# Spreading a row factor with GpSimd's partition broadcast, after the product, in the x3 stage of a four-layer kernel

## The chip, the cores and the metric

The kernel runs on one core of a Trainium2 chip. The core has five engines with a queue of instructions each: TensorE (PE; its weight loads are listed apart as PEld), VectorE (DVE), ScalarE (ACT), GpSimd (POOL) and SyncE (SP), which here only issues transfers. Sixteen DMA engines carry out the transfers. Data is worked on in SBUF, 128 partitions wide; TensorE writes its products to PSUM, from which VectorE and ScalarE read.

The metric is the device time of one execution in microseconds (us). Before the change the median of three runs is 3373.68 us, from 3369.82 to 3382.41.

## The reference, cut to what matters

The input is x, 256 x 256 tokens of 128 channels in fp32. Four layers follow one another, each of the form x = x + layer(group_norm(x)): an attention over rows, a triangle product with 16 channels, a triangle product with 128 channels, and a convolution. The change lies in the third, layer 2:

```python
zn = _layernorm(z, ln_in_w, ln_in_b)
a = jax.nn.sigmoid(zn @ Wga + bga) * (zn @ Wla + bla)
b = jax.nn.sigmoid(zn @ Wgb + bgb) * (zn @ Wlb + blb)
k = jnp.einsum('bimc,bmjc->bijc', a, b)
out = jax.nn.sigmoid(zn @ Wgo + bgo) * (_layernorm(k, ln_o_w, ln_o_b) @ Wlo + blo)
```

Here z is the group-normalised x2 (x after two layers), and x3 = x2 + out. The last line is what the changed stage computes. A layer norm takes a mean and a factor (one over the standard deviation) per token. The kernel folds the subtraction of the token's mean, and the norm's weights, into the weight matrices; what is left for each token is a subtraction of the group norm's mean per channel, and a multiplication by one number per token.

## The kernel before, in words

Activations are kept in HBM with channels as rows: x2T, kD and x3T are 128 rows of 65,536 tokens. The work is done in 32 blocks of SC = 2048 tokens (1 MB), each in two halves of H2 = 1024, each half in two pieces of CK = 512, the width of one product in PSUM. Every stage is written under manual scheduling: each engine gets its instructions in the order of the program text, and a tile pool with n buffers makes the writer of a tile wait for the last reader of the tile n before it.

Layer 2 has three stages. The first (p5, lines 1091 to 1230) makes a and b, the row rs2D of token factors, and, for the last two blocks only, the finished gates (`gates`). The second (p6, lines 1251 to 1288) multiplies them into kD, collecting the sums of k and of k squared in k1 and k2. The third, called the x3 stage here (p7, lines 1292 to 1394), is the one that is changed. For each block s it

- loads k (`load7k`, four buffers) and x2 (`load7x`, seven buffers in two pools);
- spreads two rows of factors over the 128 partitions with `broadcast_rows`: four matmuls with K = 32, whose weights pick row s out of a tile that holds all blocks' factors as [32 c + s, 512]; the rows are rs2 (factor of z, `normalise_z`) and rk (factor of k, `normalise_k`). The spread rows stand in PSUM, in the pool psX, which has two buffers of two banks;
- multiplies them in on VectorE: lines 1318 (z, with the mean m2 subtracted first) and 1310 (k);
- takes the gate product on TensorE and its sigmoid on ScalarE (`gate7`, three blocks ahead of use, AHEAD = 3), then the product of k (`product7`), both into the pool psM with two buffers of two banks;
- multiplies gate and product on VectorE (line 1379), adds x on GpSimd (line 1392), sums x3 and its square on ScalarE for the next group norm (`sums7`, lines 1338 and 1339) and stores the block (`finish7`, line 1344).

In iteration s the order on TensorE is: gate product of block s + 3, half 0; k product of block s, half 0; z broadcast of block s + 4; gate product, half 1; k product, half 1; k broadcast of block s + 1. VectorE follows it with the gate times product of half 0, the z multiplies, the gate times product of half 1, and the k multiplies. GpSimd has one addition of the whole block. The sync queue issues the load of k for block s + 3, the load of x for block s + 5 and the store of block s - 1, in that order; the x load reuses the buffer of block s - 2. Blocks 30 and 31 have their gates already, so from iteration 26 on there is no z broadcast, and from 27 on no gate product.

Ahead of the loop come the z multiplies of blocks 0 to 3, the root and reciprocal of k's variance (lines 1350 to 1355), its way through HBM into rk (lines 1356 to 1358), the gates of blocks 0 to 2 and the first k multiply.

Of the kernel before, what the change touches and what calls it, by code (L numbers as in the profile page):

```python
# [2 lines left out]

# [5 lines left out]

F32 = mybir.dt.float32  # L10
AF = mybir.ActivationFunctionType
ALU = mybir.AluOpType
# [4 lines left out]
P = 128  # L17
# [3 lines left out]
SC = 2048  # L21
NSC = T // SC
CK = 512
# [9 lines left out]
def kernel(ctx: ExitStack, tc: tile.TileContext, a: dict, out: bass.AP):  # L33
    nc = tc.nc
# [22 lines left out]
    rs2D = dram.tile([1, T], F32, name="rs2D")  # L57
# [13 lines left out]
    const = ctx.enter_context(tc.tile_pool(name="const", bufs=1))  # L71
# [20 lines left out]
    for sign, base in ((1, 0), (-1, 3)):  # L92
# [2 lines left out]
            pattern=[[-4 * sign, 32], [0, 4]], channel_multiplier=sign,  # L95
        )
    gmat = gmat.rearrange("p a b -> p (a b)")
    epst = const.tile([P, 1], F32, name="epst")
    nc.vector.memset(epst, EPS)

# [45 lines left out]
    b2w = const.tile([P, 6], F32, name="b2w")  # L146
# [91 lines left out]
    with tc.tile_pool(name="x0", bufs=1) as xres, tc.tile_pool(name="p0", bufs=3) as sb:  # L238
        held = {s: xres.tile([P, SC], F32, name=f"x0_{s}") for s in range(RES, NSC)}
        with tc.tile_pool(name="p0ps", bufs=3, space=PSUM) as ps, tc.tile_pool(  # L240
            name="f0ps", bufs=2, space=PSUM
# [167 lines left out]
        with tc.tile_pool(name="p1", bufs=2) as wk_sb, tc.tile_pool(  # L409
            name="p1ps", bufs=4, space=PSUM  # L410
# [8 lines left out]
            with tc.manual_schedule():  # L419
# [5 lines left out]
                for i, s in enumerate(order):  # L425
# [4 lines left out]
                    for c in range(4):  # L430
                        nc.tensor.matmul(
                            pr[32 * c : 32 * c + 32, :], lhsT=wt, rhs=xc[:, c * CK : (c + 1) * CK],
                            start=True, stop=True,
# [17 lines left out]
                    while len(sums) > (i < NSC - 1):  # L451
                        j, sq = sums.pop(0)
                        for c in range(4):
                            nc.tensor.matmul(
                                e2[32 * c : 32 * c + 32, :], lhsT=slide[:, 31 - j : 63 - j],
                                rhs=sq[:, c * CK : (c + 1) * CK], start=(j == order[0]), stop=(j == order[-1]),
# [24 lines left out]
    with tc.tile_pool(name="p2e", bufs=6) as eb, tc.tile_pool(name="p2c", bufs=1) as cs:  # L481
        triT = cs.tile([P, NH, 2, N], F32, name="triT")
        with tc.tile_pool(name="p2", bufs=2) as sb, tc.tile_pool(
            name="p2S", bufs=2, space=PSUM
        ) as psS, tc.tile_pool(name="p2z", bufs=1, space=PSUM) as psZ, tc.tile_pool(
            name="p2M", bufs=3, space=PSUM
# [183 lines left out]
            rb = psS.tile([P, 2, CK], F32, name="p2i_rb", tag="p2_S")  # L670
            for c in range(2):
                nc.tensor.matmul(
                    rb[:, c, :], lhsT=sel[32 * c : 32 * c + 32, 0:1].to_broadcast([32, P]),
                    rhs=rs0[32 * c : 32 * c + 32, :], start=True, stop=True,
# [173 lines left out]
    with x1_scope:  # L848
        with tc.tile_pool(name="p3", bufs=3) as sb, tc.tile_pool(
            name="p3ps", bufs=3, space=PSUM  # L850
# [15 lines left out]
            for i, s in enumerate(order1):  # L866
                p1 = ps.tile([P, CK], F32, name="p3_1")
                p2 = ps.tile([P, CK], F32, name="p3_2")
                for pp, w in ((p1, v1), (p2, v2)):
                    for c in range(4):  # L870
                        nc.tensor.matmul(
                            pp[32 * c : 32 * c + 32, :], lhsT=w, rhs=xs[s][:, c * CK : (c + 1) * CK],
                            start=True, stop=True,
# [18 lines left out]
        with tc.tile_pool(name="z", bufs=2) as sb, tc.tile_pool(  # L892
            name="zps", bufs=3, space=PSUM
# [28 lines left out]
            at = turn_z(0)  # L922
            for k in range(16):
                nxt = turn_z(k + 1)
                pz = tri_multiply(nc, ps, at, AB[k // 2][1], k % 2).rearrange("p t n -> p (t n)")
                at = nxt
# [32 lines left out]
        with tc.tile_pool(name="p4", bufs=3) as sb, tc.tile_pool(  # L959
            name="p4psg", bufs=2, space=PSUM  # L960
        ) as psg, tc.tile_pool(name="p4psz", bufs=2, space=PSUM) as psz, tc.manual_schedule():
            zs, gts, sums = {}, {}, []
# [42 lines left out]
            for i, s in enumerate(order):  # L1005
# [5 lines left out]
                for c in range(4):  # L1011
# [3 lines left out]
                        start=True, stop=True,  # L1015
# [54 lines left out]
    with tc.tile_pool(name="f2", bufs=1) as sb, tc.tile_pool(name="f2ps", bufs=1, space=PSUM) as ps:  # L1070
        po = ps.tile([P, 1], F32, name="f2_o")
        nc.tensor.matmul(po, lhsT=ones, rhs=mr2neg, start=True, stop=True)
        nc.vector.tensor_scalar(off2, po, 1.0 / D, None, ALU.mult)

    H2 = 2 * CK

    def broadcast_rows(psX, rows, s, name, tag="x"):


        rb = [psX.tile([P, 2, CK], F32, name=name, tag=tag) for _ in range(2)]  # L1080
        for c in range(4):
            nc.tensor.matmul(  # L1082
                rb[c // 2][:, c % 2, :], lhsT=sel[32 * c : 32 * c + 32, s : s + 1].to_broadcast([32, P]),
                rhs=rows[32 * c : 32 * c + 32, :], start=True, stop=True,
            )
        return [t.rearrange("p c t -> p (c t)") for t in rb]
# [4 lines left out]
    rs2_scope = ExitStack()  # L1091
# [140 lines left out]

    rk_pool = rs2_scope.enter_context(tc.tile_pool(name="rk", bufs=1))
    x7_pool = rs2_scope.enter_context(tc.tile_pool(name="x7", bufs=3))
    z7_pool = rs2_scope.enter_context(tc.tile_pool(name="z7", bufs=2))
    rk = rk_pool.tile([P, CK], F32, name="rk")
    rs2 = rk_pool.tile([P, CK], F32, name="rs2_")
    for c in range(4):
        nc.gpsimd.dma_start(  # L1239
            rs2[32 * c : 32 * c + 32, :], rs2D.rearrange("o (s c t) -> c (o s) t", c=4, t=CK)[c]  # L1240
        )
    k1 = rk_pool.tile([P, 2 * N], F32, name="k1")
    k2 = rk_pool.tile([P, 2 * N], F32, name="k2")
    xs7 = {}
# [1 line left out]
    def load7x(s, pool, bufs):  # L1246
        if s < NSC:
            xs7[s] = pool.tile([P, SC], F32, name="p7_x", bufs=bufs)
            nc.sync.dma_start(xs7[s], x2T[:, s * SC : (s + 1) * SC])

    with tc.tile_pool(name="p6", bufs=3) as sb, tc.tile_pool(name="p6ps", bufs=3, space=PSUM) as ps:
        nc.vector.memset(k1, 0.0)
# [41 lines left out]
    with tc.tile_pool(name="p7", bufs=2) as sb, tc.tile_pool(name="p7psX", bufs=2, space=PSUM) as psX, tc.tile_pool(  # L1294
        name="p7psM", bufs=2, space=PSUM
    ) as psM, tc.manual_schedule():
        ks, zns, gts = {}, {}, dict(gates)
        AHEAD = 3

        def load7k(s):  # L1300
            if s < NSC:
                ks[s] = sb.tile([P, SC], F32, name="p7_k", bufs=4)
                nc.sync.dma_start(ks[s], kD[:, s * SC : (s + 1) * SC])

        def normalise_k(s):
            if s < NSC:
                rb = broadcast_rows(psX, rk, s, "p7_rk")
                for h in range(2):
                    hs = slice(h * H2, (h + 1) * H2)
                    nc.vector.tensor_tensor(ks[s][:, hs], rb[h], ks[s][:, hs], ALU.mult)  # L1310

        def normalise_z(s):
            if s < NSC and s not in gates:
                rb = broadcast_rows(psX, rs2, s, "p7_rz")
                zns[s] = z7_pool.tile([P, SC], F32, name="p7_zn")
                for h in range(2):
                    hs = slice(h * H2, (h + 1) * H2)
                    nc.vector.scalar_tensor_tensor(
                        zns[s][:, hs], xs7[s][:, hs], m2, rb[h], ALU.subtract, ALU.mult
                    )  # L1320

        def product7(src, w, h):
            pm = psM.tile([P, 2, CK], F32, name="p7_pm")
            for c in range(2):
                k = 2 * h + c
                nc.tensor.matmul(pm[:, c, :], lhsT=w, rhs=src[:, k * CK : (k + 1) * CK], start=True, stop=True)  # L1326
            return pm.rearrange("p c t -> p (c t)")

        def gate7(s, h):
            if s < NSC and s not in gates:  # L1330
                if h == 0:
                    gts[s] = sb.tile([P, SC], F32, name="p7_g", bufs=5)
                nc.scalar.activation(
                    gts[s][:, h * H2 : (h + 1) * H2], product7(zns[s], wf2[:, 4, :], h), AF.Sigmoid, bias=b2w[:, 4:5]
                )

        def sums7(x, junk, i):
            nc.scalar.activation(junk, x, AF.Identity, bias=m2neg, accum_out=g1[:, i : i + 1])
            nc.scalar.activation(junk, x, AF.Square, bias=m2neg, accum_out=g2[:, i : i + 1])

        def finish7(s):
            x = xs7.pop(s)
            sums7(x, gts.pop(s), s)
            nc.sync.dma_start(x3T[:, s * SC : (s + 1) * SC], x)

        load7k(0)
        load7x(3, sb, 4)
        normalise_z(0)

        nc.vector.scalar_tensor_tensor(k1, k1, -1.0 / D, k1, ALU.mult, ALU.mult)  # L1350
        nc.vector.tensor_tensor(k2, k2, k1, ALU.add)
        nc.vector.tensor_scalar(k2, k2, 0.0, None, ALU.max)
        nc.scalar.activation(k2, k2, AF.Sqrt, bias=epst, scale=1.0 / D)
        normalise_z(1)
        nc.vector.reciprocal(k1, k2)
        nc.sync.dma_start(rkD.rearrange("o (p t) -> p (o t)", p=P), k1)
        for c in range(4):
            nc.sync.dma_start(rk[32 * c : 32 * c + 32, :], rkD.rearrange("o (s c t) -> c (o s) t", c=4, t=CK)[c])
        for s in range(1, 3):
            load7k(s)  # L1360
        load7x(4, sb, 4)
        gate7(0, 0)
        gate7(0, 1)
        normalise_z(2)
        gate7(1, 0)
        gate7(1, 1)
        normalise_z(3)
        gate7(2, 0)
        gate7(2, 1)
        normalise_k(0)  # L1370
        for s in range(NSC):
            load7k(s + 3)
            load7x(s + 5, *((x7_pool, 3) if (s + 5) % 7 < 3 else (sb, 4)))
            last = s == NSC - 1
            for h in range(2):
                hs = slice(h * H2, (h + 1) * H2)
                gate7(s + AHEAD, h)
                pl = product7(ks[s], w2[:, 5, :], h)
                nc.vector.scalar_tensor_tensor(gts[s][:, hs], pl, b2w[:, 5:6], gts[s][:, hs], ALU.add, ALU.mult)  # L1379
                if h == (s + AHEAD not in gates and s + AHEAD < NSC):  # L1380
                    normalise_k(s + 1)
                if h == 0:
                    normalise_z(s + AHEAD + 1)
                if last:
                    nc.vector.tensor_tensor(xs7[s][:, hs], xs7[s][:, hs], gts[s][:, hs], ALU.add)
                    if h == 0:
                        finish7(s - 1)
                    sums7(xs7[s][:, hs], gts[s][:, hs], s + h)
                    nc.sync.dma_start(x3T[:, s * SC + h * H2 : s * SC + (h + 1) * H2], xs7[s][:, hs])
            del ks[s]  # L1390
            if not last:
                nc.gpsimd.tensor_tensor(xs7[s], xs7[s], gts[s], ALU.add)  # L1392
                if s:
                    finish7(s - 1)
# [486 lines left out]
```

## Time and profile before

| what | value |
|---|---|
| median of three runs | 3373.68 us (3369.82 to 3382.41) |
| profiled execution, first to last instruction (its own time and its span are this one figure) | 3369.3 us |
| TensorE busy, whole span | 3117.7 us, 93% |
| VectorE, ScalarE, GpSimd busy | 2268.5, 2019.0, 1593.4 us |
| mean granted TensorE clock | 0.962 |
| HBM traffic | 458.35 MB read, 287.64 MB written |
| x3 stage: first z broadcast, first product of the loop, last sum | 2628.34, 2650.33, 2939.5 us |
| x3 stage, 2750 to 2800 us: PE, DVE, ACT, POOL busy | 50.00, 38.01, 33.45, 22.72 of 50 us |

The page of the profile shows one execution on the chip. Line numbers are those of the kernel before. A group of instructions reads: line, engine, operation, written tile <- read tiles, shapes, count, then busy time, mean time of one in ns, and the engine's idle time just before them with what ended it. In the profile's names digits that follow a letter's prefix are left out, so p7_rz is p_rz, p7_pm is p_pm and p7_x is p_x; names such as p_x and p_pm occur in other stages as well. An fp32 product appears as two matmul records of 512 columns, so a half of a block (two products) is four, and the four broadcast matmuls are eight, which run side by side on four groups of 32 rows. The chain of work that ended last is followed backwards from the last instruction, at each step to what released it.

### The profile page before, as it was taken

How to read it: one execution, taken by the hardware profiler on the slowest of the kernel's cores; microseconds unless marked ns; L12 is line 12 of the kernel's file. 1: busy time of each engine (PE TensorE's matmuls, PEld its weight loads, DVE VectorE, ACT ScalarE, POOL GpSimd, SP SyncE). 2: the span in 40 equal slices, each digit the busy share in tenths (PEclk: the TensorE clock that was granted, in tenths of full speed). 3: DMA queues.
4: the chain of work that ended last, by engine and by line, in shares of the span. 5: the costliest groups of instructions: out<-in, count | busy, mean ns of one | idle time of the engine just before them, and what ended most of it. 6: DMA issues, size and time to landing. Idle time of an engine off the chain costs nothing. (4 is left out here: it accounts for less than half of the span.)

```text
span 3369.3 us, 52577 instructions
## 1 busy us (share of the span) xinstructions
PE 3117.7 (93%) x20274; PEld 1644.3 (49%) x20274; DVE 2268.5 (67%) x2612; ACT 2019.0 (60%) x2209; POOL 1593.4 (47%) x878
## 2 busy tenths in 40 slices
PE   6669999999999999967997999999999999769998
PEld 5415555555555555523432444445999433224444
DVE  5627888888888888853555455444555677758776
ACT  3657777777777777734686444443444466636565
POOL 4146777777777777720483000001555344414444
PEclk8889999999999999988997999999999999979999
DMA  9972333333333333369597768666999899756764
GB/s 395 366 292 81 121 109 121 108 121 109 120 109 117 112 113 116 108 262 351 196 408 306 264 244 315 244 237 254 350 352 352 305 335 332 283 159 201 211 188 132
DMA packets 297977, 749.51 MB, mean 222 GB/s; under 512 B 74585, under 2 KB 145195, under 8 KB 248571
## 3 DMA queue, kind: packets, MB, share of 16 engines
q1 hardware_dynamic: 289659, 735.24, 61.2%
q0 software_dynamic: 7776, 9.81, 0.9%
q8 instruction: 162, 2.65, 0.3%
q10 hardware_dynamic: 288, 1.05, 0.1%
q14 instruction: 92, 0.75, 0.1%
HBM read 458.35 MB, written 287.64 MB: 221 GB/s over the span
## 5 line engine op out<-in xcount | busy, mean ns | idle before, releaser
L564 DVE TENSOR_TENSOR p_e<-p_S,triT 128x1024 f32<-128x1024 f32 x512 | 609.3, 1212 | 144.4 <-PE p_S L554 144.4
L574 POOL TENSOR_TENSOR p_es<-p_e 128x1024 f32<-128x1024 f32 x256 | 603.5, 2368 | 125.3 <-issue 65.3
L572 ACT ACTIVATE p_e<-p_e,mbT 128x1024 f32<-128x1024 f32 x512 | 551.8, 1137 | 61.4 <-DVE p_e L564 61.3
L1167 PE MATMUL p_pm<-p_zn,wf 128*128 128x512 f32 x1040 | 449.6, 593 | 2.1 <-ACT p_a L1202 1.9
L539 PE MATMUL p_mm<-p_xn,w 128*128 128x512 f32 x768 | 405.3, 611 | 0.3 <-DVE p_v L534 0.3
L1167 PEld LDWEIGHTS p_pm<-p_zn,wf 128*128 128x128 f32 x1040 | 196.5, 190 | 255.3 <-issue 246.1
L554 PE MATMUL p_S<-p_q,p_k 32*128 32x256 f32 x4096 | 295.4, 400 | 3.5 <-DVE p_e L564 3.3
L1575 POOL TENSOR_TENSOR p_q<-p_q,p_pb 128x2024 f32<-128x2024 f32 x32 | 144.2, 4506 | 254.3 <-DVE p_pb L1569 254.3
L554 PEld LDWEIGHTS p_S<-p_q,p_k 32*128 32x128 f32 x4096 | 185.9, 184 | 159.5 <-PE p_mm L530 91.7
L1839 PE MATMUL tp_z<-p_B,tp_at 128*128 128x256 f32 x1024 | 250.5, 388 | 0.8 <-DMA p_B<-bD 0.5
L587 PE MATMUL p_o<-p_e,p_v 128*32 128x256 f32 x4096 | 248.6, 383 | 0.0
L513 POOL TENSOR_TENSOR p_xn<-p_xn,p_rs 128x1024 f32<-128x1024 f32 x63 | 151.4, 2403 | 205.5 <-DMA p_rb<-rzD 114.2
L1239 POOL DMA_DIRECT2D rs__17906<-rs2D x4 | 2.0, 510 | 506.5 <-DVE p_zn L1160 506.5
L1282 POOL TENSOR_TENSOR k<-k,p_sq 128x512 f32<-128x512 f32 x128 | 163.2, 1275 | 156.8 <-ACT p_sq L1280 156.8
L1392 POOL TENSOR_TENSOR p_x<-p_x,p_g 128x2048 f32<-128x2048 f32 x30 | 136.4, 4547 | 160.4 <-DVE p_g L1379 87.4
L1839 PEld LDWEIGHTS tp_z<-p_B,tp_at 128*128 128x128 f32 x1024 | 185.1, 191 | 23.2 <-DVE tp_at L1830 1.6
L539 PEld LDWEIGHTS p_mm<-p_xn,w 128*128 128x128 f32 x768 | 126.0, 190 | 104.6 <-issue 88.5
L1281 DVE TENSOR_TENSOR k<-tp_z,k 128x512 f32<-128x512 f32 x128 | 88.6, 692 | 127.1 <-ACT p_sq L1280 127.1
L587 PEld LDWEIGHTS p_o<-p_e,p_v 128*32 128x32 f32 x4096 | 120.3, 110 | 110.3 <-ACT p_g L545 41.5
L1278 ACT COPY p_K<-tp_z 128x512 f32<-128x512 f32 x128 | 75.1, 587 | 157.9 <-PE tp_z L1839 157.9
L545 ACT ACTIVATE p_g<-p_mm,bgh 128x512 f32<-128x512 f32 x128 | 88.0, 687 | 131.4 <-PE p_mm L539 131.3
L530 PEld LDWEIGHTS p_mm<-w,p_xn 128*128 128x128 f32 x1024 | 134.4, 191 | 61.1 <-issue 60.4
(379 smaller groups left out, 5892.7 us busy)
## 6 DMA issues: line engine op xcount, KB each, us to landing
p_x<-x2T SPq DMA_DIRECT2D x60, 1024.0 KB
x<-x1T SPq DMA_DIRECT2D x51, 1024.0 KB
p_x<-in_x_dram SPq DMA_DIRECT2D x32, 1024.0 KB
p_x<-xT SPq DMA_DIRECT2D x64, 512.0 KB
x2T<-x SPq DMA_DIRECT2D x32, 1024.0 KB
aD<-p_a SPq DMA_DIRECT2D x32, 1024.0 KB
bD<-p_b SPq DMA_DIRECT2D x32, 1024.0 KB
p_A<-aD SPq DMA_DIRECT2D x32, 1024.0 KB
```

Of the source, the lines that this page charges most:

```text
L513: nc.gpsimd.tensor_tensor(xn, xn, groups[g]["rs"], ALU.mult)
L539: nc.tensor.matmul(pm, lhsT=w, rhs=t["xn"][:, cs_], start=True, stop=True)
L554: nc.tensor.matmul(Ss[h // 2][:, h % 2, u, :], lhsT=t["k"][hp, r * N + u * P : r * N + (u + 1) * P], rhs=t["q"][hp, r * N : (r + 1) * N], ...
L564: nc.vector.tensor_tensor(e[:, :, 2 * p : 2 * p + 2, :].rearrange("p u h n -> p h u n"), Ss[p], triT[:, 2 * p : 2 * p + 2, :, :], ALU.add,)
L572: nc.scalar.activation(e[:, u, :, :], e[:, u, :, :], AF.Exp, bias=mbT[:, u, i : i + 1])
L574: nc.gpsimd.tensor_tensor(es, e[:, 0, :, :], e[:, 1, :, :], ALU.add)
L587: nc.tensor.matmul(t["o"][hp, r % 2, :], lhsT=t["v"][:, r * 2 + u, hp], rhs=e[:, u, h, :], start=(u == 0), stop=(u == 1),)
L1167: nc.tensor.matmul(pm[:, c, :], lhsT=wf2[:, i, :], rhs=zns[s][:, k * CK : (k + 1) * CK], start=True, stop=True)
L1282: nc.gpsimd.tensor_tensor(k2, k2, sq, ALU.add)
L1392: nc.gpsimd.tensor_tensor(xs7[s], xs7[s], gts[s], ALU.add)
L1575: nc.gpsimd.tensor_tensor(q[:, :, 1 : N - 2], q[:, :, 1 : N - 2], pb[:, :, 0 : N - 3], ALU.add)
L1839: nc.tensor.matmul(pz[:, t, :], lhsT=at[:, u, t * P : (t + 1) * P], rhs=Bc[:, u, :], start=(u == 0), stop=(u == 1))
```

## The change

The z factor is no longer spread by TensorE and no longer multiplied onto x before the gate product. The gate product now takes x2 as it was loaded. The factor row of a block is loaded as one row of 2048 numbers into partition 0, 32, 64 or 96 of the tile rs2 (`row7`), right behind the load of x; GpSimd's partition broadcast writes it to all 128 partitions of a tile rbs in SBUF (`spread_z`, two buffers). VectorE then computes (product + gcol) times the spread row into a tile zg, and ScalarE takes the sigmoid from there. gcol is the product of the gate weights with the negative mean, one column, made once ahead of the x2 stage by one more matmul and copy.

The k factor is still spread by TensorE, but now in `spread_k` right after the k product of half 0, and the two halves are multiplied separately: half 0 behind the first gate times product of an iteration, half 1 behind the second.

The row tile no longer comes by four GpSimd transfers of the whole factor tile. A library with the partition broadcast is loaded to GpSimd near the start of the kernel, ahead of the weights' transfers. In the start of the stage the k statistics now come before anything else on VectorE, since no z multiply stands ahead of them.

```diff
     gmat = gmat.rearrange("p a b -> p (a b)")
+    nc.gpsimd.load_library(library_config.all_libraries[10])
...
+        pg = ps.tile([P, 1], F32, name="f2_g")
+        nc.tensor.matmul(pg, lhsT=wf2[:, 4, :], rhs=m2neg, start=True, stop=True)
+        gcol = const.tile([P, 1], F32, name="gcol")
+        nc.vector.tensor_copy(gcol, pg)
...
-    z7_pool = rs2_scope.enter_context(tc.tile_pool(name="z7", bufs=2))
-    rs2 = rk_pool.tile([P, CK], F32, name="rs2_")
-    for c in range(4):
-        nc.gpsimd.dma_start(
-            rs2[32 * c : 32 * c + 32, :], rs2D.rearrange("o (s c t) -> c (o s) t", c=4, t=CK)[c]
-        )
+    rs2 = rk_pool.tile([P, SC], F32, name="rs2_")
+
+    def row7(s):
+        at = 32 * (s % 4)
+        return rs2[at : at + 1, :]
...
             nc.sync.dma_start(xs7[s], x2T[:, s * SC : (s + 1) * SC])
+            nc.sync.dma_start(row7(s), rs2D[:, s * SC : (s + 1) * SC])
...
-        def normalise_k(s):
+        def spread_k(s):
             if s < NSC:
-                rb = broadcast_rows(psX, rk, s, "p7_rk")
-                for h in range(2):
-                    hs = slice(h * H2, (h + 1) * H2)
-                    nc.vector.tensor_tensor(ks[s][:, hs], rb[h], ks[s][:, hs], ALU.mult)
-
-        def normalise_z(s):
+                rks[s] = broadcast_rows(psX, rk, s, "p7_rk")
+
+        def normalise_k(s, h):
+            if s < NSC:
+                hs = slice(h * H2, (h + 1) * H2)
+                nc.vector.tensor_tensor(ks[s][:, hs], rks[s][h], ks[s][:, hs], ALU.mult)
+
+        def spread_z(s):
             if s < NSC and s not in gates:
-                rb = broadcast_rows(psX, rs2, s, "p7_rz")
-                zns[s] = z7_pool.tile([P, SC], F32, name="p7_zn")
-                for h in range(2):
-                    hs = slice(h * H2, (h + 1) * H2)
-                    nc.vector.scalar_tensor_tensor(
-                        zns[s][:, hs], xs7[s][:, hs], m2, rb[h], ALU.subtract, ALU.mult
-                    )
+                rbs[s] = sb.tile([P, SC], F32, name="p7_rb")
+                nc.gpsimd.partition_broadcast(rbs[s], row7(s))
...
         def gate7(s, h):
             if s < NSC and s not in gates:
+                hs = slice(h * H2, (h + 1) * H2)
                 if h == 0:
                     gts[s] = sb.tile([P, SC], F32, name="p7_g", bufs=5)
-                nc.scalar.activation(
-                    gts[s][:, h * H2 : (h + 1) * H2], product7(zns[s], wf2[:, 4, :], h), AF.Sigmoid, bias=b2w[:, 4:5]
-                )
+                pg = product7(xs7[s], wf2[:, 4, :], h)
+                zg = sb.tile([P, H2], F32, name="p7_zg")
+                nc.vector.scalar_tensor_tensor(zg, pg, gcol, rbs[s][:, hs], ALU.add, ALU.mult)
+                nc.scalar.activation(gts[s][:, hs], zg, AF.Sigmoid, bias=b2w[:, 4:5])
...
-        normalise_z(0)
+        spread_z(0)
+        spread_z(1)
...
-        normalise_z(1)
...
-        gate7(0, 0)
-        gate7(0, 1)
-        normalise_z(2)
-        gate7(1, 0)
-        gate7(1, 1)
-        normalise_z(3)
-        gate7(2, 0)
-        gate7(2, 1)
-        normalise_k(0)
+        for s in range(3):
+            gate7(s, 0)
+            gate7(s, 1)
+            if s < 2:
+                spread_z(s + 2)
+        spread_k(0)
+        normalise_k(0, 0)
+        normalise_k(0, 1)
...
-                if h == (s + AHEAD not in gates and s + AHEAD < NSC):
-                    normalise_k(s + 1)
                 if h == 0:
-                    normalise_z(s + AHEAD + 1)
+                    spread_k(s + 1)
+                    spread_z(s + AHEAD + 1)
+                normalise_k(s + 1, h)
```

More of the change, by code (lines that the diff above doesn't have):

```diff
@@ L5 @@
 import concourse.tile as tile
-from concourse import mybir
+from concourse import library_config, mybir
 from concourse.masks import make_identity
@@ L1296 @@
     ) as psM, tc.manual_schedule():
-        ks, zns, gts = {}, {}, dict(gates)
+        ks, rks, rbs, gts = {}, {}, {}, dict(gates)
         AHEAD = 3
```

## The prediction

> **What bounds the kernel now.** I began with the row of 40 slices on the page, to see which engine is full where, and with the chain of work that ended last. The x3 stage runs from about 2628 to 2939 us of the 3369.3 us span, slices 32 to 35 (of 84.2 us). The lines are TensorE (PE) and DMA busy tenths:
>
> ```profile
> PE   6669999999999999967997999999999999769998
> ...
> DMA  9972333333333333369597768666999899756764
> ```
>
> In those slices TensorE stands at 9, and the DMA engines at 8, 9, 9, 7: two candidates. The chain, asked for a stretch in the middle of the stage (start, length, what), decides:
>
> ```profile
> 2744.42 3.63 PE p_pm L1326 x8
> 2748.05 1.07 PE p_rz L1082 x8
> 2749.12 3.63 PE p_pm L1326 x8
> 2752.75 1.07 PE p_rk L1082 x8
> 2753.82 3.63 PE p_pm L1326 x8
> ```
>
> No other engine and no transfer appears in it: it is TensorE's own instructions back to back. One block of 2048 tokens takes 3.63 + 1.07 + 3.63 + 1.07 = 9.40 us: two pairs of products (gate and k, one pair per half) and two row broadcasts, one of the z factor (p_rz), one of the k factor (p_rk). The windows view of the same stage (busy us of PE, PEld, DVE, ACT, POOL, then clock, DMA share, GB/s; the last line is an earlier stage):
>
> ```profile
> 2750.00:2800.00 50.00, 50.00 (x171) 18.73 (x173) 38.01 (x33) 33.45 (x32) 22.72 (x5) 1.00 0.94 340
> ...
> 1684.00:1769.00 85.00, 84.27 (x281) 31.09 (x280) 49.26 (x74) 70.72 (x69) 70.14 (x23) 1.00 1.01 409
> ```
>
> TensorE is busy for 50.00 of 50 us at full clock. VectorE has 24% free, GpSimd half. DMA is 94% busy but moves only 340 GB/s, where the same queue moved 409 GB/s in the earlier stage, with its megabyte loads and stores; so I do not read 0.94 as full. The groups of the stage (line, engine, tiles, count, busy, mean ns, idle before and why) give the prices:
>
> ```profile
> L1392 POOL TENSOR_TENSOR p_x<-p_x,p_g 128x2048 f32<-128x2048 f32 x25 | 113.6, 4545 | 147.9 <-DVE p_g L1379 75.0 <-DMA x3T<-p_x 72.9
> ...
> L1379 DVE SCALAR_TENSOR_TENSOR p_g<-p_pm,b2w,p_g 128x1024 f32<-128x1024 f32 x51 | 65.5, 1284 | 56.1 <-PE p_pm L1326 56.1
> L1318 DVE SCALAR_TENSOR_TENSOR p_zn<-p_x,gn_mean,p_rz 128x1024 f32<-128x1024 f32 x50 | 61.6, 1273 | 0.0
> L1310 DVE TENSOR_TENSOR p_k<-p_rk,p_k 128x1024 f32<-128x1024 f32 x52 | 61.0, 1214 | 2.3 <-PE p_rk L1082 2.3
> L1333 ACT ACTIVATE p_g<-p_pm,b2w 128x1024 f32<-128x1024 f32 x52 | 58.0, 1114 | 83.7 <-PE p_pm L1326 83.0
> ```
>
> VectorE's and ScalarE's idle time ends in a TensorE product: both wait for TensorE. And the sync queue's loads and stores of one block, from the order of time:
>
> ```profile
> 2752.78 0.32 SPq L1303 DMA_DIRECT2D p_k<-kD  x1
> 2756.32 0.32 SPq L1249 DMA_DIRECT2D p_x<-x2T  x1
> 2758.86 0.32 SPq L1344 DMA_DIRECT2D x3T<-p_x  x1
> ```
>
> **What the Trainium skill says.** "GPSIMD Engine Reference", section 3.1, gives 4497 ns for a two-input add at 2048 fp32 elements; L1392 shows 4545 ns, so it agrees. The same section gives 1.03 cycles an element at 1.2 GHz for short one-input loops; no run here shows one of this size. Its section 2.1 adds about 6 us at the first call of a freshly loaded library; not shown here either. "SBUF — State Buffer", section on the two sides, says that GpSimd and VectorE exclude each other only when VectorE reads two SBUF inputs or runs a two-port mode. The trace agrees as far as it goes: L1379 reads PSUM and SBUF, and takes 1.28 us beside a running L1392 as well as without. The new VectorE instruction has that form too.
>
> **The change part by part.**
>
> *z broadcasts on TensorE, removed.* In the loop normalise_z ran for s + 4 below 30, so in 26 iterations, each 1.07 us of the chain. A block falls from 9.40 to 8.33 us: 26 x 1.07 = 27.8 us. Cover is needed from every other resource below 8.33 us a block:
>
> *VectorE.* Two L1318 go, two scalar_tensor_tensor of PSUM product, column and spread row come, the same form at about 1.28 us. Sum per block 2 x (1.28 + 1.28 + 1.21) = 7.54 us; 0.8 us free. Order matters more: products alternate between two PSUM buffers, and now VectorE frees all of them. Laying out one block from 0: gate product 0 to 1.81, k product to 3.62, k broadcast to 4.69, gate to 6.50, k to 8.31. VectorE's second gate multiply then starts at 6.6 and ends at 7.9; its buffer is wanted at 8.31. The second k multiply ends at 9.75; its buffer is wanted at 10.1. It fits with 0.4 us to spare; if lost, what is late is the next gate product, by the difference. k's halves are scaled half a block earlier than used, so the 0.42 us for which weight loads waited on L1310 is gone too, without worth.
>
> *ScalarE.* The sigmoid moves behind VectorE. ScalarE spends 2 x 1.11 on it and 2 x 2.19 on the sums, 6.6 us a block; gates are made three blocks ahead, so a later sigmoid delays nobody.
>
> *GpSimd.* One broadcast of 2048 elements joins the 4.55 us add. No row shows it. From below: the one-input rate, 2048 x 1.03 / 1.2 GHz = 1.8 us (estimate). From above: a two-input pass over the same tile, 4.55 us. I take 2.5 us: one pass, plus handing the row from core to core. 4.55 + 2.5 = 7.05, under 8.33, so hidden; from 3.8 us up it isn't. It is queued between two adds: behind it wait the next add, the x3T store and, through the sync queue, the x load. The row for block s + 4 is asked for one iteration before its broadcast and used one iteration after, which leaves over a microsecond.
>
> *DMA.* Thirty-two row loads of 8 KB go onto the sync queue, 0.32 us of issue each, three of them before the stage, under the products of p6; the four GpSimd loads of rs2 (L1239, 2.0 us in all, long before use) go. In a block the queue issues 4 x 0.32 = 1.3 us. Data per block 3.15 MB: at 8.33 us that is 378 GB/s, above today's 340, below 409 (7.7 us). The sync queue is in order: the x load waits until an x3T store has landed and ScalarE's sums have left its buffer, and behind it stand the row load and the next store. In before a store is issued at 2749.5 (one block ahead of 2758.86) and the x load that waits for it at 2756.3, under 7 us; that loop fits in 8.33 us, barely. x has more slack than before: its first reader is the gate product, half a block later than L1318 was. Cost nothing; both ends for the range: 0, and the DMA rival below.
>
> *Start of the stage.* Before: first z broadcast at 2628.34, two z multiplies ahead of the k statistics on VectorE, reciprocal at 2636.18, four z broadcasts among six gate products, loop entered at 2650.33. After: the statistics come first; the chain is last GpSimd sum 2628.98, k2 add 0.69, max 0.43, root 0.72, reciprocal 3.34, so the first gate multiply at about 2634.6. Its first two products are long done by then (slow clock: eight passes in 5.85 us there). Four more at about 1.8 to 2.4, and the k broadcast at 1.07, give loop entry near 2645.5. Gain 4.5 us; 2 if the first broadcast pays 6 us.
>
> *End of the stage.* From block 27 on there is no gate; k halves are now apart, so the second gate of block 27 comes some 0.6 us earlier than at 2910.4 and the GpSimd adds behind it follow. Gain 0.5.
>
> *Elsewhere.* One product and copy for gcol before the x2 stage: 0.3 us lost. The library load stands ahead of the weights' DMAs on GpSimd at 3.4 us; the tightest weights (the w2 columns, issued by 52.5) are first read at 67 us, so 6 us hides; without that cover it would cost as much as it exceeds 12.
>
> Sum: 27.8 + 4.5 + 0.5 - 0.3 = 32.5 us. From the profiled 3369.3: 3336.8. The median of the runs shown, 3373.7, is 4.4 above that execution, so 3341 for a median.
>
> **The rivals.**
>
> *DMA becomes the bound.* For: 0.94 busy now. If that is truly full, 340 / 0.94 = 362 GB/s, 8.7 us a block, 26 x 0.7 = 18 us, and with the start and about 3 us of loads in advance some 23; with 350 GB/s, 9.0 us and 15. 3350 to 3359. Against: 409 GB/s above.
>
> *GpSimd becomes the bound.* A broadcast of 4.55 us gives 9.1 us a block: 26 x 0.3 = 8, with a start gain of 2: 3364. For: nothing in the trace prices it. Against: it reads one row and has one input.
>
> *Slower: the broadcast is a slow cross-partition operation.* It decides from 9.40 - 4.55 = 4.85 us per row. The skill's GPSIMD page, section 3.2, has a reduction over partitions of this size at 247.7 us (no run here shows it). At 10 us a block takes 14.55 us: 26 x 5.15 = 134 us more, 3508. Against: a copy has no arithmetic across partitions.
>
> *The change does not do what it says:* TensorE would still issue p_rz; the diff leaves it no such instruction in this stage. No chance given.
>
> **How the numbers follow.** Sum as worked out (a block at 8.3 to 8.5 us): 0.70, its own range 3332 to 3350, being 26 x 0.17 = 4 us on one side and the start's 2 us and the spread of the runs (3369.8 to 3382.4) on both. DMA: 0.13. GpSimd bound: 0.09. Slow broadcast: 0.08. The bound of same is 0.5%, 17 us, about what a measurement of this kernel can tell from no change. Faster: 0.70 and most of the DMA case, 0.79. Same: its rest and the GpSimd case, 0.13. Slower: 0.08. The range reaches from 3329 over the DMA case to 3364, at the GpSimd case.
>
> **What would show it.** Right: chain of 3.63 and 1.07 with only p_rk, starts of L1326 pairs repeating every 8.33 us; GpSimd under 7.5 us a block; 375 GB/s or more; loop entry at about 17 us from the first product. Wrong: TensorE waiting for VectorE's gate multiply (buffers), VectorE for the spread row (GpSimd), or products for x (DMA); or the first 100 us, or GpSimd's L574 in the attention, longer than before.

## The result

The changed kernel is slower. Its median is 3427.68 us (3423.35 to 3430.35), beside 3374.31 us (3369.82 to 3382.41) for the kernel before on the same chip: a ratio of 1.0139, 95% interval 1.0102 to 1.0175. The forecast was 3341 us.

The profiled execution has a span of 3421.6 us, 52.3 more than before. Two marks divide it: the last store of k at the end of p6, and the first instruction of the group norm behind the x3 stage.

| stretch | before, us | after, us | difference |
|---|---|---|---|
| start to the last k store | 2627.1 | 2640.2 | +13.1 |
| x3 stage, to the group norm's statistic | 312.9 | 354.4 | +41.5 |
| from there to the end | 429.3 | 427.0 | -2.3 |

The 40 slices of the page of after (TensorE and DMA busy tenths, slices of 85.5 us), in answer to the same two lines of before:

```profile
PE   5669999999999999967996999999999987759998
...
DMA  9982333333333333378697676767998877756764
```

In slices 32 to 35, those of the stage, TensorE stands at 9, 8, 7, 7 and DMA at 8, 7, 7, 7. In before they were 9, 9, 9, 7 and 8, 9, 9, 7: TensorE had a 7 in slice 35 then too, in which the stage ends, and not 9 throughout as the prediction read it. In slices 33 and 34 neither is full any more. The windows view of after (busy us of PE, PEld, DVE, ACT, POOL, then clock, DMA share, GB/s) has one stretch near the start of the loop and one a little later:

```profile
2663.00:2687.00 24.00, 24.00 (x72) 9.34 (x71) 21.17 (x18) 12.45 (x11) 16.84 (x6) 1.00 0.92 342
2703.00:2763.00 60.00, 47.02 (x123) 17.95 (x122) 38.49 (x32) 34.95 (x35) 37.99 (x11) 0.92 0.77 263
```

In the first, TensorE is busy for 24.00 of 24 us. In the second for 47.02 of 60, and the DMA engines move 263 GB/s at a share of 0.77. Something changed in between. The chain of the work that ended last shows what (start, length, what; the kernel after):

```profile
2664.77 7.07 PE p_pm L1329 x16
2671.84 1.07 PE p_rk L1087 x8
...
2690.72 10.37 DMA x3T<-p_x
...
2701.17 0.32 SPq L1254
...
2701.87 11.21 DMA x3T<-p_x
```

The first two lines are what was forecast: the products of a block and one broadcast, 7.07 + 1.07, 8.13 us from block to block, with the z broadcast gone. From 2690.72 on the chain is a transfer, the store of x3, then the load of x that waits for it, and the next store, which takes 11.21 us. TensorE is no longer in it. The groups of the stage after (line, engine, tiles, count, busy, mean ns, idle before and why) clear the compute engines:

```profile
L1339 DVE SCALAR_TENSOR_TENSOR p_zg<-p_pm,gcol,p_rb 128x1024 f32<-128x1024 f32 x60 | 76.9, 1283 | 78.6 <-PE p_pm L1329 74.2 <-POOL p_x L1396 4.4
...
L1323 POOL PARTITION_BROADCAST p_rb<-rs__17908 x30 | 68.7, 2294 | 103.7 <-DMA rs__17908<-rs2D 62.2 <-DMA p_x<-x2T 32.9 <-DVE p_zg L1339 4.6
```

The new broadcast takes 2.29 us, VectorE's new form 1.28. GpSimd idles for transfers, VectorE for TensorE, and TensorE for 52.6 us for the x load. The order of time on the sync queue shows the change of regime (start, issue time, transfer; L1254 loads x, L1349 stores x3, L1309 loads k):

```profile
2681.54 0.32 SPq L1254 DMA_DIRECT2D p_x<-x2T  x1
...
2682.60 0.32 SPq L1349 DMA_DIRECT2D x3T<-p_x  x1
...
2689.94 0.32 SPq L1254 DMA_DIRECT2D p_x<-x2T  x1
...
2690.72 0.32 SPq L1349 DMA_DIRECT2D x3T<-p_x  x1
2692.84 0.32 SPq L1309 DMA_DIRECT2D p_k<-kD  x1
2701.17 0.32 SPq L1254 DMA_DIRECT2D p_x<-x2T  x1
...
2701.87 0.32 SPq L1349 DMA_DIRECT2D x3T<-p_x  x1
...
2713.13 0.32 SPq L1254 DMA_DIRECT2D p_x<-x2T  x1
```

At 2681.54 the x load goes out 1.06 us ahead of the store. The store of 2690.72 then has the x load and the k load in flight beside it, and lands 10.37 us later. The x load of 2701.17 needs that landing, because it reuses the buffer that the store reads. And the next store, 2701.87, stands behind the x load in the queue, though its data were ready: GpSimd's addition had ended at 2698.85. From there x load, store and k load (the latter at 2702.30) go out within 1.2 us, and nothing more is issued until the store has landed: a round of 11.96 us here, 11.7 on average over the 22 rounds from 2701.17 to the last x load at 2958.51. I call this the lock. What the sync queue waits for in the stage (us in total, times, longest), after:

```profile
SPq L1254 <- DMA x3T<-p_x: 235.5, 25, 10.6
```

and before:

```profile
SPq L1249 <- DMA x3T<-p_x: 39.7, 25, 2.7
SPq L1249 <- ACT p_g L1339: 39.6, 25, 3.0
```

Before, an x load waited 39.7 / 25 = 1.6 us for the store and then another 1.6 us for ScalarE's sums. The queue came to that wait when the k load had gone out (2752.78 + 0.32, with the store ahead of it at 2749.45), so the store had landed about 3.7 + 1.6 = 5.3 us after its issue. After, it waits 9.4 us on average, nearly always for the store.

In the first 13.1 us of the difference the start of the kernel has a part. In the kernel after GpSimd waits without a releaser that the profile shows, ahead of the identity matrix:

```profile
11.13 0.28 POOL masks.py:199 TENSOR_SCALAR_AFFINE_SELECT ident<-ident 128x128 f32<-128x128 f32 x1 [9.96 <-issue]
```

A second such wait, 5.00 us long, ends at 18.29, where the new library is loaded. TensorE's first transposes wait for that identity, until 11.47 us, where before they began at 6.00:

```profile
11.47 4.99 PE L336 MATMUL p_t<-ident,p_x 128*128 128x128 f32 x24 [11.47 <-POOL ident masks.py:199]
```

### The profile page after: what moved, and what is told of

Its sections match the earlier page's. It is cut to its first block, busy times and chain, and to the rows that moved or that the text cites. A ratio compares the mean times of both kernels' runs of the same rounds, so it can differ in the third digit from the quotient of the medians.

```text
span 3421.6 us, 52156 instructions
## 1 busy us (share of the span) xinstructions
PE 3105.4 (91%) x20036; PEld 1648.5 (48%) x20036; DVE 2273.1 (66%) x2613; ACT 2021.0 (59%) x2209; POOL 1659.4 (48%) x904
## 3 DMA queue, kind: packets, MB, share of 16 engines
q10 hardware_dynamic: 288, 1.05, 0.1%
## 5 line engine op out<-in xcount | busy, mean ns | idle before, releaser
L1329 PE MATMUL p_pm<-p_x,wf 128*128 128x512 f32 x240 | 131.2, 677 | 58.8 <-DMA p_x<-x2T 52.6
L588 PEld LDWEIGHTS p_o<-p_e,p_v 128*32 128x32 f32 x4096 | 120.0, 109 | 109.3 <-ACT p_g L546 41.5
```

The lines of the kernel that those rows point to most:

```text
L588: nc.tensor.matmul(t["o"][hp, r % 2, :], lhsT=t["v"][:, r * 2 + u, hp], rhs=e[:, u, h, :], start=(u == 0), stop=(u == 1),)
```

## The experiments

Two theories stood first. Theory Q: the in-order sync queue, in which a load that waits for a store's landing holds up the next store. Theory R: the 32 row loads. For the start, theory L: the library load is on the path.

**The row loads left out, all but four.**

```diff
-            nc.sync.dma_start(row7(s), rs2D[:, s * SC : (s + 1) * SC])
+            if s < 4:
+                nc.sync.dma_start(row7(s), rs2D[:, s * SC : (s + 1) * SC])
```

> The changed kernel, but only the first four factor rows are loaded; the 28 later row loads are left out, so later blocks are multiplied with old rows. Theory Q (the sync queue locks: the x load waits for the store of the block before, that store stands behind the x load, and all transfers of a block run together, so that the store lands last): the rows are a small part of it, the loop still locks at 11 to 12 us a block, time 3410 to 3425. Theory R (the single-partition row load holds up one DMA engine, which runs on alone for some 2.5 us in each block): without the rows the loop goes at 8.1 to 8.5 us a block, time 3345 to 3360 (the 13 us lost ahead of the stage stay).

3428.52 us, ratio 1.0152 (1.0133 to 1.0172), as slow as after; the sync queue waits 233.1 us in 24 waits for x3 stores, as in after. Theory R falls as the reason for the loss.

**The store ahead of the x load.**

```diff
             load7k(s + 3)
-            load7x(s + 5, *((x7_pool, 3) if (s + 5) % 7 < 3 else (sb, 4)))
...
                 if s:
                     finish7(s - 1)
+            load7x(s + 5, *((x7_pool, 3) if (s + 5) % 7 < 3 else (sb, 4)))
```

> The changed kernel, with the loads of x and of the row issued after the store of the same iteration instead of before it; nothing left out. Theory Q: the store no longer stands behind the x load, so it lands before the next x load needs it; 8.1 to 8.6 us a block, 3345 to 3365. Theory R: the row still holds up an engine and the store with it; 10 us a block or more, 3390 or more.

3349.67 us, ratio 0.9932 (0.9909 to 0.9955): faster than before, with the same work and the same engines as after. The sync queue of this kernel (L1349 stores x3, L1254 loads x, L1309 loads k) and its windows view late in the stage:

```profile
2716.88 0.32 SPq L1349 DMA_DIRECT2D x3T<-p_x  x1
2717.30 0.37 SPq L1254 DMA_DIRECT2D p_x<-x2T  x1
```

```profile
2800.00:2850.00 50.00, 50.00 (x148) 19.75 (x148) 44.14 (x37) 39.46 (x38) 41.73 (x13) 1.00 1.01 389
```

The store goes out when GpSimd has made its data; no x load stands in front of it. The x load behind it needs the store of one block earlier, which has had 8 us more. Blocks repeat every 8.13 us to the end, TensorE is full again, the transfers run at 389 GB/s and a share of 1.01. The stage takes 277.8 us, 35.1 less than before (27.8 + 4.5 + 0.5 = 32.8 were forecast).

**The same reordering in the kernel before** (the edit is the same).

> The kernel before, with nothing but the x load issued after the store of the same iteration. Theory Q: TensorE sets the pace at 9.40 us, the order of the transfers does nothing: within 5 us of before. Rival (part of what e2_store_first gained is the order itself): more than 8 us faster.

3378.53 us, ratio 1.0001 (0.9986 to 1.0016): no difference. At 9.40 us a block TensorE bounds it, and the queue's order costs nothing on top.

**The library load alone, added to before.**

```diff
+    nc.gpsimd.load_library(library_config.all_libraries[10])
```

> The kernel before, with nothing but the library load added near the start. If the library costs what the trace after shows ahead of the x3 stage, the first transposes start some 5.5 us later, and p6 ends some 13 us later: 3387 against 3374. If those 13 us come from something else in the change, the time stays within 5 us.

3384.86 us, ratio 1.0017 (1.0003 to 1.0031): by the medians some 8 us. In its profiled execution the first transposes begin at 12.45 us and the last k store is issued at 2639.4, 12.3 us later than in before. From profile to profile the library load alone thus brings nearly all of the 13.1. The profiled execution of before, with a span of 3369.3 us, is one of its faster ones; the medians compare all of them.

**The library load moved into p5, in the reordered kernel**, with and without a load of the standard library at the very end.

```diff
-    nc.gpsimd.load_library(library_config.all_libraries[10])
...
         for s in range(7):
             load5(s)
+        nc.gpsimd.load_library(library_config.all_libraries[10])
...
                 emit(s - 2)
+        nc.gpsimd.load_library(library_config.standard)
```

> The changed kernel with the store ahead of the x load (as in e2_store_first), the library load moved from the kernel's start to the first x2-stage loads, where GpSimd has nothing to do for some 500 us, and the standard library loaded again after GpSimd's last instruction. Theory L (two library loads are paid at the start: the standard one, because the last execution left the other resident, and then the new one): both are hidden now, the first transposes start at 6 us again, and the time is 8 to 12 us under e2_store_first, 3337 to 3342. Rival: the standard library's load at the start comes from the program holding a second library at all, or the reload at the end is not hidden: 3345 to 3350.

> As e7_library_hidden, but without the reload at the end. Theory L: the standard library must be loaded at the start, which holds the identity matrix until some 11 us, so most of the start's loss stays: 3345 to 3350. Rival (the second load, ahead of the weights, was what cost time): 3337 to 3342.

3343.79 us, ratio 0.9897 (0.9877 to 0.9917), with the last line; 3346.02, ratio 0.9908 (0.9884 to 0.9932), without it. These two can't be told apart, and their intervals overlap that of the reordered kernel (0.9909 to 0.9955), so what moving the load is worth is not settled. The start shows a mechanism, though. With the last line the transposes begin at 6.02 us again. Without it GpSimd waits 9.23 us ahead of the identity, although that kernel loads no library until p5: the standard library comes back at the start of an execution when another was left loaded by the one before, as these two kernels, which differ in that line alone, show. Yet in both kernels the last k store is issued at about 2639 us, some 12 us later than before, and with the last line 6.8 of them are there by the first store of x1 (324.4 against 317.6), ahead of any library. So the loss ahead of the x3 stage is not accounted for by those waits alone, and where it comes from is open.

**The row loads alone, added to before**, into a tile that nothing reads.

```diff
+            nc.sync.dma_start(rows7[at : at + 1, :], rs2D[:, s * SC : (s + 1) * SC])
```

> The kernel before, with nothing but the 32 row loads added, into a tile that nothing reads. Theory Q: in the slower rhythm of 9.40 us the store has landed before the x load needs it, rows or not: within 10 us of before. Theory R: each block gains 1 to 2.5 us of waiting for the held-up engine: 3395 to 3440.

3378.14 us, ratio 1.001 (0.9996 to 1.0025): no difference. But the runs spread from 3368.93 to 3411.99, and the profiled one shows why. Its sync queue (L1250 loads x, L1347 stores x3):

```profile
2775.91 0.32 SPq L1250 DMA_DIRECT2D p_x<-x2T  x1
...
2778.43 0.32 SPq L1347 DMA_DIRECT2D x3T<-p_x  x1
...
2786.51 0.32 SPq L1250 DMA_DIRECT2D p_x<-x2T  x1
...
2787.82 0.32 SPq L1347 DMA_DIRECT2D x3T<-p_x  x1
...
2797.72 0.32 SPq L1250 DMA_DIRECT2D p_x<-x2T  x1
```

Up to here the x load stands 2.5 us ahead of the store and a block takes 9.40 us. At 2786.51 an x load comes 1.2 us late and stands 1.3 us ahead of the store; that store lands late, and the next x load comes at 2797.72, 11.2 us on. The lock can thus be entered at the old pace too, and then it stays to the end of the stage. Two of the 20 runs (3394.87 and 3411.99) lie above all 27 runs of before beside them (up to 3387.63); whether the row loads make the lock likelier is not shown.

**What brings the lock about.** Theory Q said: the shorter block. To see it I slowed TensorE, with broadcast matmuls that nothing reads.

```diff
+                if h == 1 and s + AHEAD + 1 < NSC - 2:
+                    broadcast_rows(psX, rk, s, "p7_rk")
```

> The changed kernel, with four broadcast products of the k row added in each iteration that nothing reads, so that TensorE needs about 9.2 us a block again; nothing left out. Theory Q with the pace as its trigger: at 9.2 us the store lands in time, no lock, and the time is that of before plus the library's 8 us, less some of the start of the stage: 3375 to 3390. Rival (the lock comes from something else in the change: where the k halves, the row or GpSimd's broadcast stand): it locks at 11 to 12 us a block as after: 3415 to 3430.

3427.99 us, ratio 1.0157 (1.0132 to 1.0182). The added matmuls did not run as I had priced them: TensorE needs 10.58 us a block and is the chain alone until 2875, so this time says little. What the x loads of its sync queue wait for in the stage (us in total, times, longest) says more:

```profile
SPq L1254 <- DMA x3T<-p_x: 155.5, 24, 10.3
```

Up to 2788.45 the x loads come 10.4 to 10.8 us apart, 0.8 to 1.1 us ahead of the store. From 2800.02 on they stand 0.7 us ahead of it, wait for the store before, and come 10.0 to 11.9 us apart, until the wait is on the chain as well. So this kernel locks too, at a longer block than that of before. Half as many matmuls:

```diff
+                if h == 1 and s + AHEAD + 1 < NSC - 2:
+                    extra = psX.tile([P, 2, CK], F32, name="p7_ex", tag="x")
+                    for c in range(2):
+                        nc.tensor.matmul(extra[:, c, :], lhsT=sel[0:32, 0:1].to_broadcast([32, P]), rhs=rk[0:32, :], start=True, stop=True)
```

> The changed kernel with two unneeded broadcast matmuls per iteration (about 1.1 us of TensorE), so that TensorE needs about 9.2 us a block, near the 9.40 of before; the run with four of them needed 10.58 us of TensorE alone and told nothing of the queue. Theory Q, that the shorter period brings the x load up against the store: at 9.2 the x load, released about 7 us after the store before it, goes out 2 us ahead of the next store, whose transfer then lands within the block; blocks of 9.2 to 9.4, no long waits of the sync queue for x3T stores, time 3376 to 3390 (that of before, the library's 8 added, 4 off at the start of the stage). Rival P, that other parts of the change (row loads, GpSimd's broadcasts, k in halves) make the queue lock at any pace: blocks of 11 to 12, 3420 to 3435.

3419.27 us, ratio 1.0131 (1.011 to 1.0152). From the chain in the first half of the stage (p_ex are the added matmuls):

```profile
2717.91 1.91 PE p_ex L1387 x4
```

The two cost 1.91 us, so a block took 3.63 + 1.07 + 3.63 + 1.91 = 10.24. Even so, from 2763.87 on the x loads come 11.2 to 12.1 us apart, with the queue waiting for stores. The expectation was missed twice, in the pace and in the lock: a shorter block is not needed for it. In this kernel the x load stands only 1.05 us ahead of the store (2733.15 and 2734.20), as in after, however long the block is. That is another thing which the change does. The sums that must leave x's buffer stand behind the second sigmoid on ScalarE, and the sigmoid now waits for VectorE.

**The shorter block alone, in the kernel before**: no z broadcast from block 4 on.

```diff
-                rb = broadcast_rows(psX, rs2, s, "p7_rz")
+                rb = broadcast_rows(psX, rs2, s, "p7_rz") if s < 4 else last_rk
```

> The kernel before with the z broadcasts of TensorE left out from block 4 on (z is multiplied by the row last spread for k, so the output is another one): no library, no row load, no GpSimd broadcast, k not in halves; TensorE needs 8.33 us a block. Theory Q, the shorter period alone brings the lock: blocks start at 8.33 and go to 11 or 12 within a few blocks, with the sync queue waiting for x3T stores, 3400 to 3425. Rival P, that it takes other parts of the change: 8.3 to 8.5 us through the stage, 3341 to 3350.

3402.46 us, ratio 1.0066 (1.0043 to 1.009). It has none of the change's row loads, GpSimd broadcasts or library, and it locks. Its sync queue (L1249 loads x, L1346 stores x3):

```profile
2707.02 0.32 SPq L1346 DMA_DIRECT2D x3T<-p_x  x1
...
2714.29 0.32 SPq L1249 DMA_DIRECT2D p_x<-x2T  x1
2715.60 0.32 SPq L1346 DMA_DIRECT2D x3T<-p_x  x1
...
2724.93 0.32 SPq L1249 DMA_DIRECT2D p_x<-x2T  x1
2725.34 0.38 SPq L1346 DMA_DIRECT2D x3T<-p_x  x1
...
2736.45 0.32 SPq L1249 DMA_DIRECT2D p_x<-x2T  x1
```

At 8.58 us a block the x load keeps 2.6 us ahead of the store for a while (2704.40 ahead of 2707.02), with the DMA share at 0.99. Then a store takes 7.3 us, the next 9.3, the next 11.1. So the shorter block is enough, without the rest of the change.

**The sums ahead of the second sigmoid**, in the kernel after and in the one with 10.24 us a block.

```diff
+                if h == 1 and s and not last:
+                    sums7(xs7[s - 1], gts.pop(s - 1), s - 1)
                 gate7(s + AHEAD, h)
...
                 if s:
-                    finish7(s - 1)
+                    nc.sync.dma_start(x3T[:, (s - 1) * SC : s * SC], xs7.pop(s - 1))
```

> The changed kernel with ScalarE's sums of a block ahead of the second sigmoid of the iteration, not behind it: the x load, which waits for them, is released about 2.5 us earlier, so some 2.7 us ahead of the store instead of 1.1. Theory Q (the shorter period lets transfers queue up until a store lands too late for the next x load, wherever x stands ahead of it): it locks all the same, after some blocks, as the kernel before without z broadcasts did, 3400 to 3428. Rival S, that it is the changed kernel's late sums, which put the x load right ahead of the store: no lock, 8.13 us a block, 3346 to 3354.

> The same order of ScalarE in the kernel paced by two unneeded matmuls (10.24 us of TensorE a block, where the lock came in the middle of the stage). Theory Q with S as a second part: x stands some 2.7 us ahead of the store and the longer period leaves the transfers time, so no lock, 10.24 us a block to the end, about 3395 to 3405 (3374, 26 blocks x 0.84 more, 8 for the library, 4 off at the start). If the sums' place does not matter: the lock as before, 3415 to 3422.

At the pace of after: 3424.24 us, ratio 1.0115 (1.0078 to 1.0152), locked from 2712 on. At 10.24 us: 3400.64, ratio 1.0061 (1.0042 to 1.0079), and no lock. The sync queue of the latter (L1254 loads x, L1404 stores x3):

```profile
2781.21 0.37 SPq L1254 DMA_DIRECT2D p_x<-x2T  x1
...
2786.85 0.32 SPq L1404 DMA_DIRECT2D x3T<-p_x  x1
```

The x load stands 5.6 us ahead of the store (2.7 were expected), and all blocks take 10.24 us. Two parts of the change are thus each enough for the lock: the shorter block whatever the order of the sums, and, with the rest of the change in place, the later sums even at a long block. Neither is needed, as the kernel before with the row loads added showed. Of the edits tried, only the order of the queue removes it at 8.13 us. What makes the one store late with which it begins is not shown.

## Why the prediction was wrong

**z broadcasts on TensorE removed: right.** The chain has p_rk alone, and 8.13 us a block where 8.33 was worked out. In the reordered kernel this lasts to the end.

**VectorE, ScalarE, GpSimd: right as costs.** VectorE's new form takes 1.28 us as taken; the broadcast 2.29 us where 2.5 was chosen between 1.8 and 4.55; 4.55 + 2.29 = 6.84 us of GpSimd fits under a block. That 2.5 came so near, between ends so far apart, is luck. The rivals of a slow broadcast and of GpSimd as the bound fall. But the step on ScalarE, that "a later sigmoid delays nobody", is wrong: it looked at the gates, and not at what is queued behind the sigmoid. The sums are, and for them waits the x load.

**DMA: the step that failed**, at "that loop fits in 8.33 us, barely" and "Cost nothing". The step had the loop right, store, landing, x load, next store, and its place in the queue. It read the "under 7 us" from the issue of a store to the x load as the time that a store takes. It was not: the store had landed after 5.3 us, and ScalarE's sums ended the wait. And it took that time for fixed, though the runs show it to depend on what is in flight beside the store. The Trainium skill's page "DMA: Bandwidth & Descriptors", in the section "Anatomy of one DMA", gives 2.0 us plus the bytes over 436 GB/s, for a transfer that GpSimd issues; carried over to the sync queue's megabyte that is an estimate of 4.4 us alone, against 5.3 in before. With the x load and the k load issued next to it, the same store took 10.37 and then 11.2 us. 11.2 + 0.7 for the two issues is a round of 11.9 us. The 22 rounds took 257.3 us, where 22 of the forecast's blocks of 8.33 take 183.3; that is 74 us more, and less the 33 that were forecast as gained, 41, where 41.5 were measured. The match is luck in part, for smaller terms, such as a block of 8.13 instead of 8.33 ahead of the lock, cancel in it. The reordered kernel gives the loss without a sum: its stage takes 277.8 us, that of after 354.4. The page also says that a wait is made by the issuing sequencer ahead of the dispatch, not by the DMA engines; that is the mechanism by which a waiting load held up a store with which it has nothing to do. The trace agrees: 235.5 us of waits, all on the sync queue. The prediction had named the sign: "products for x (DMA)"; TensorE waited 52.6 us for them.

**The rival "DMA becomes the bound" fell as well.** Bandwidth was not short: 263 GB/s in the lock, 389 without it. The loss was of the same place but of another kind, latency in a chain, and no rival had it. The share of before, 0.94 at 340 GB/s, was rightly not taken for full.

**Elsewhere: too low.** "6 us hides" looked at the first reader of the weights. Two waits came, not one: 9.96 us ahead of the identity, and 5.00 us at the new library. The Trainium skill's page "GPSIMD Engine Reference", section 2.1, has about 6 us at the first call of freshly loaded code. Here the 5.00 us stood at the load, and all 30 broadcasts, the first included, took 2.29 to 2.30 us. The first wait holds up the identity and with it the first transposes, by 5.5 us. The library load alone cost 8 us by the medians and moved the last k store by 12.3 us in the profile. That it does so through these waits is not shown: with both of them gone from the start, the last k store still came 11.5 us late.

**Start of the stage: nearly right.** The loop was entered 18.6 us after the first product (2660.00 against 2641.42) instead of 17. The first gate multiply began at 2648.05, when the reciprocal on VectorE (to 2647.99) and GpSimd's first broadcast (from 2645.71 to 2648.02) had both ended; from there to the loop it took 11.95 us, where 2634.6 to 2645.5, or 10.9, were worked out.

With the queue reordered and the library moved, the kernel takes 3343.79 us, within 3 us of the forecast for the change as it was made. The gain was real and was lost in the queue. That the number comes so near is luck in part: in its profiled execution the stage gains 35.8 us and the stretch ahead of it loses 11.5, where 32.8 and 0.3 were forecast.

## What to carry to other kernels

When a queue carries both the stores and the loads that reuse their buffers, follow one round of it (issue, landing, next issue) at the new pace and with everything else that will be in flight, and put each store ahead of the load that waits for an earlier one. Where a wait in the profile has two releasers, split it before using its length: the one that ended it hides how much room the other has. When an instruction is put behind a slower producer, ask what is queued behind that instruction on its own engine.

## What the runs showed of the hardware

- A 1 MB store landed 5.3 us after its issue in before; issued within 1.2 us of two 1 MB loads it took 11.2. Between two such rounds of after, from 2723.5 to 2726.0, the DMA engines stood at a share of 0.09 or less and moved 33 GB/s or less, which is about one of the sixteen at work, by an estimate (1/16 = 0.06). Without the row loads it was the same (0.08 or less from 2742.5 to 2744.5).
- A mix of loads and stores of 1 MB held 389 GB/s at a share of 1.01 in the reordered kernel; 0.94 went with 340 GB/s in before. At 10.24 us a block it was 0.91 with 307 ahead of the lock (2690 to 2750), and 0.80 with 310 when the sums came first (2680 to 2900). The share alone doesn't tell what room is left.
- Two broadcast matmuls with K = 32 on the same group of 32 rows took 1.91 us, four on four groups 1.07. The Trainium skill's page "TensorE: Matmul & The Clock Gate", part 3, has a gain of 3.07 from four row groups with K = 32 and 512 columns; here, in fp32, it is 4 x 0.955 / 1.07 = 3.6.
- A partition broadcast of one row of 2048 fp32 to 128 partitions took 2.29 us on GpSimd.
- With another GpSimd library than the standard one left loaded at the end of an execution, GpSimd waited 9 to 11 us at the start of the next (9.23, 9.96 and 10.94 us ahead of the identity); with the standard library loaded last that wait was gone, and the identity was made at 1.45 us. By their medians these kernels, 3343.79 and 3346.02 us, can't be told apart.
